# Softmax sums of each four heads in a tile of their own, and their reciprocals written behind the copies of the transposes

## The chip, the core and the metric

The kernel runs on one core of a Trainium2 chip. The metric is the device time of one execution in microseconds (us). Executions of one kernel agree within 0.2% here, most within 0.1%. A single core has no second die to compare with, and all runs below are of the fast state, so times can be set beside each other. Ratios are those of the runs of one round on one chip: the mean time of one kernel's fast runs over the mean of the other's, so they are not quite the ratios of the medians that are quoted.

The engines are called by the profile's short names in its lines: PE is TensorE (PEld its weight loads), DVE VectorE, ACT ScalarE, POOL GpSimd. PSUM is the memory that the matmuls and transposes here write into; the kernel takes it in pieces called banks. The granted clock (PEclk) is the share of its full clock that the profile shows TensorE being given, as a mean over the stretch named.

## The reference, cut to what matters

The first layer is a state-space layer, which the change leaves alone. The second is attention in a 7 x 7 neighbourhood, 12 heads of 32 channels, on a 64 x 64 image, four images:

```python
logits = jnp.stack([jnp.einsum('bnchw,bnchw->bnhw', q, k_pad[..., di:di + H, dj:dj + W])
                    for di in range(ws) for dj in range(ws)], axis=-1)
logits = logits + rel_bias.reshape(nh, ws * ws)[None, :, None, None, :]
attn = jax.nn.softmax(logits, axis=-1)
out = jnp.einsum('bnhwk,bnkchw->bnchw', attn, v_win).reshape(B, C, H, W)
```

The kernel works on blocks of 8 x 16 pixels (128 queries), whose neighbourhoods lie in a window of 14 x 22 = 308 keys. A mask in the bias leaves each query its 49 keys.

## The kernel before

A *turn* handles one group of four heads in one block; there are 4 images x 8 stripes x 4 blocks x 3 groups = 384 turns. What a turn does:

```python
def scores(b, s, bl, m, blk):
    sg = w2.tile([P, 4, NK], F32, tag="sg", ..., bufs=4)
    mx = w2.tile([P, 4], F32, tag="mx", ...)
    for hh in range(4):
        ...
        nc.tensor.matmul(lg[:, :NK], ...)                       # logits into PSUM
        nc.vector.tensor_tensor_reduce(                         # bias, negation, and the maximum
            sg[:, hh, :], lg[:, :NK], bias[:, 4 * m + hh, :], -1.0, BIG,
            ALU.add, ALU.min, mx[:, hh : hh + 1])
        act(sg[:, hh, :], sg[:, hh, :], AF.Exp, scale=-1.0, bias=mx[:, hh : hh + 1],
            accum_out=blk["sum"][:, 4 * m + hh : 4 * m + hh + 1])   # ScalarE: exponential and its sum
    return sg

def normalised(m, sg, blk):
    rs = w2.tile([P, 4], F32, tag="rsum", name="rsum")
    nc.vector.reciprocal(rs, blk["sum"][:, 4 * m : 4 * m + 4])
    for hh in range(4):
        nc.gpsimd.tensor_scalar(sg[:, hh, :], sg[:, hh, :], rs[:, hh : hh + 1], None, ALU.mult)

def weighted(m, sg, blk):
    ta = []
    for pair in range(2):
        pt = bank(ps_t, "pt")                                    # ps_t has two banks
        ...                                                      # four transposes, 128 x 110
        t = w2.tile([P, 4, P], F32, tag="ta", name="ta", bufs=4)
        nc.vector.tensor_copy(...)                               # VectorE empties the bank: "the copies"
        ta.append(t)
    pt = bank(ps_t, "pt")                                        # needs the first bank again
    ...                                                          # four transposes, 128 x 88: "the third set"
    nc.scalar.copy(...)                                          # ScalarE empties it
    return ta, tb
```

The turns overlap. While the scores of group n are made, group n-1 is normalised and group n-2 transposed:

```python
blk["sum"] = w2.tile([P, NH], F32, tag="sum", ..., bufs=3)       # once a block of three groups
for m in range(NJ):
    sg = scores(b, s, bl, m, blk)
    if turned is not None:
        attend()                                                 # attention times values, group n-3
    turned = None
    if pending:
        normalised(*pending[-1][:3])                             # group n-1
    if len(pending) > 1:
        pm, psg, pblk, *rest = pending.pop(0)
        turned = (pm, *weighted(pm, psg, pblk), pblk, *rest)     # group n-2
    pending.append((m, sg, blk, bl, b, s, aT))
    ...                                                          # a piece of the next stripe's projections
```

In this layer the source's order is not the order of the queues: the framework's scheduler sorts each engine's instructions when the program is built.

## Time and profile before

9406.5 us. The prediction below shows the profile's lines and works from them; it takes the attention layer from 6860 us to the end. *Idle* is a stretch's length less TensorE's busy time.

Its lines are to be read from the bottom of the chain: a wait of VectorE costs time only where TensorE, which has the most to do, waits for what stands behind it.

### The profile page before, as it was taken

The numbers are of one execution on the slowest core, as the hardware profiler recorded it, in microseconds if no ns is written. First come the engines' busy times: TensorE is split into PE (matmuls) and PEld (weight loads), VectorE is DVE, ScalarE is ACT, GpSimd is POOL, SyncE is SP. The second block draws the span as 40 slices with busy tenths as digits, with TensorE's granted clock in tenths as the row PEclk, the third lists the DMA queues.
The fourth block names the chain that finished last, engine by engine and source line by source line (L and its number), as shares of the span: only waits on it lengthen the run. The fifth ranks groups of instructions, "written<-read, shape, count | busy, mean of one in ns | idle before, by whom it ended". The sixth has DMA issues, their size and how long they took to land. (4 is left out here: it accounts for less than half of the span.)

```text
span 9402.5 us, 141121 instructions
## 1 busy us (share of the span) xinstructions
PE 7733.7 (82%) x45882; PEld 5668.8 (60%) x45882; DVE 7512.0 (80%) x15604; ACT 5726.1 (61%) x13566; POOL 7641.1 (81%) x6679
## 2 busy tenths in 40 slices
PE   6877787778777887787778877887799999999998
PEld 5666666666666666666666666666554555555555
DVE  6888988898889888889898888888855555556555
ACT  5676666666666676666666666666544444444444
POOL 5898989888989898898889998999856666666666
PEclk8887888788888887788878887888699999999999
DMA  3111111111111111111111111111122222222222
GB/s 98 51 49 60 55 51 44 56 55 51 49 52 61 48 45 53 61 52 48 52 56 49 43 46 57 49 44 45 47 83 83 77 81 77 74 79 79 75 78 61
DMA packets 301925, 558.02 MB, mean 59 GB/s; under 512 B 61916, under 2 KB 185580, under 8 KB 301060
## 3 DMA queue, kind: packets, MB, share of 16 engines
q1 hardware_dynamic: 301188, 549.00, 18.6%
q8 instruction: 364, 5.96, 0.3%
q14 instruction: 373, 3.06, 0.1%
HBM read 446.33 MB, written 84.73 MB: 56 GB/s over the span
## 5 line engine op out<-in xcount | busy, mean ns | idle before, releaser
L96 ACT ACTIVATE da<-dt,nega 128x256 f32<-128x256 f32 x6144 | 2922.9, 477 | 1425.8 <-DVE hs L558 974.7
L538 POOL TENSOR_TENSOR db<-dtx,B 128x1024 f32<-128x1024 f32 x1536 | 3620.7, 2357 | 30.1
L558 DVE TENSOR_TENSOR_SCAN hp<-da,state,db 128x256 f32<-128x256 f32 x2880 | 2154.2, 748 | 303.7 <-POOL state L569 193.3
L558 DVE TENSOR_TENSOR_SCAN hs<-da,state,db 128x256 f32<-128x256 f32 x2880 | 2119.0, 736 | 341.8 <-ACT da L96 341.7
L909 POOL TENSOR_SCALAR sg<-sg,rsum 128x308 f32<-128x308 f32 x1536 | 1603.9, 1064 | 917.1 <-DVE rsum L907 771.1
L570 POOL TENSOR_TENSOR hs<-hs,C 128x512 f32<-128x512 f32 x1536 | 1951.8, 1271 | 123.2 <-POOL state L569 0.8
L578 PE MATMUL y<-ident,hv 128*128 128x128 f32 x6144 | 1191.1, 327 | 954.7 <-DVE hv L565 948.7
L578 PEld LDWEIGHTS y<-ident,hv 128*128 128x128 f32 x6144 | 850.1, 165 | 1396.3 <-DVE hv L565 1280.4
L96 ACT ACTIVATE sg<-sg,mx 128x308 f32<-128x308 f32 x1536 | 830.8, 542 | 872.7 <-DVE mx L894 840.4
L578 PE MATMUL y<-ident,hs 128*128 128x128 f32 x6144 | 1156.2, 321 | 141.5 <-POOL hs L570 140.1
L381 PE MATMUL mm_ps<-xn,w_in 128*128 128x256 f32 x4608 | 1162.6, 404 | 2.0 <-DVE xn L357 2.0
L565 DVE TENSOR_TENSOR hv<-hp,C 128x512 f32<-128x512 f32 x1536 | 1044.5, 680 | 0.0
L578 PEld LDWEIGHTS y<-ident,hs 128*128 128x128 f32 x6144 | 900.6, 169 | 189.4 <-POOL hs L570 186.0
L381 PEld LDWEIGHTS mm_ps<-xn,w_in 128*128 128x128 f32 x4608 | 924.3, 207 | 132.9 <-issue 3.0
L894 DVE CUSTOM_DVE_ANT_0 sg<-lg_ps,bias 128x308 f32<-128x308 f32 x1536 | 653.9, 474 | 270.4 <-PE lg_ps L888 270.0
L569 POOL COPY state<-hs 128x2 f32<-128x2 f32 x1536 | 289.1, 188 | 526.9 <-DVE hs L558 466.8
L388 PE MATMUL mm_ps<-xb,dcv 128*128 128x256 f32 x3072 | 716.5, 379 | 0.0
L388 PEld LDWEIGHTS mm_ps<-xb,dcv 128*128 128x128 f32 x3072 | 567.3, 190 | 72.3
L488 PE MATMUL mm_ps<-xd,w_dt 24*128 24x256 f32 x768 | 332.4, 573 | 293.5 <-DVE yg L605 290.6
L616 PE MATMUL mm_ps<-yg,w_out 128*128 128x256 f32 x2304 | 518.8, 379 | 0.0
L926 DVE COPY ta<-pt_ps 110x512 f32<-110x512 f32 x768 | 490.7, 680 | 33.4 <-PE pt_ps L921 28.4
L936 ACT COPY tb<-pt_ps 88x512 f32<-88x512 f32 x384 | 223.0, 581 | 426.8 <-PE pt_ps L932 422.7
(145 smaller groups left out, 10677.7 us busy)
## 6 DMA issues: line engine op xcount, KB each, us to landing
B<-bcrows SPq DMA_DIRECT2D x256, 512.0 KB
C<-bcrows SPq DMA_DIRECT2D x256, 512.0 KB
vw<-vd SPq DMA_DIRECT2D x1792, 33.0 KB
xr<-x SPq DMA_DIRECT2D x28, 1056.0 KB
vd<-v SPq DMA_DIRECT2D x280, 96.0 KB
xi<-in_x_dram SPq DMA_DIRECT2D x64, 384.0 KB
x<-xo SPq DMA_DIRECT2D x64, 384.0 KB
o<-x SPq DMA_DIRECT2D x96, 256.0 KB
```

The lines of the kernel that those rows point to most:

```text
L96: ins = nc.scalar.activation(o, i, func, **kw)
L381: nc.tensor.matmul(pb[:, k, :], w_in[:, j, m * P : (m + 1) * P], xn[:, j, :], start=(j == 0), stop=(j == NJ - 1),)
L388: nc.tensor.matmul(pb[:, k, :], dcv[:, d, c, :], xb[:, d, c : c + T], start=(c == 0), stop=(c == KC - 1),)
L538: nc.gpsimd.tensor_tensor(db, h["dtx"].unsqueeze(1).broadcast_to([P, NG, T]), h["bc"][g][0], ALU.mult)
L558: nc.vector.tensor_tensor_scan(to[:, k, :], da[:, k, :], db[:, 2 * half + k, :], state[:, d, n + k : n + k + 1] if I % NCHUNK else 0.0, AL ...
L565: nc.vector.tensor_tensor(hv, hp, ct[:, 0:2, :], ALU.mult)
L570: nc.gpsimd.tensor_tensor(hs, hs, ct[:, 2:4, :], ALU.mult)
L578: nc.tensor.matmul(y[:, half, :], t[:, k, half * P : (half + 1) * P], ident, is_transpose=True, start=(first and half == 0), stop=(last an ...
L616: nc.tensor.matmul(h["po", first][:, m - first, :], w_out[:, d, m * P : (m + 1) * P], h["yg"][d], start=(d == 0), stop=(d == ND - 1),)
L894: nc.vector.tensor_tensor_reduce(sg[:, hh, :], lg[:, :NK], bias[:, 4 * m + hh, :], -1.0, BIG, ALU.add, ALU.min, mx[:, hh : hh + 1],)
L909: nc.gpsimd.tensor_scalar(sg[:, hh, :], sg[:, hh, :], rs[:, hh : hh + 1], None, ALU.mult)
L926: nc.vector.tensor_copy(t[: KN[0], :, :].rearrange("p a q -> p (a q)"), pt[: KN[0], :])
```

## The change

Two things were intended. The sums of each group get a tile of their own, so that no reciprocal could be tied to another group's exponentials. And the reciprocals are written behind the transposes and copies, so that VectorE would make the copies before it waits for a sum.

```diff
+                sums = w2.tile([P, 4], F32, tag="sum", name=f"sum_{b}_{s}_{bl}_{m}", bufs=4)
@@
-                        accum_out=blk["sum"][:, 4 * m + hh : 4 * m + hh + 1],
+                        accum_out=sums[:, hh : hh + 1],
@@
-            def normalised(m, sg, blk):
+            def normalised(sg, sums):
                 rs = w2.tile([P, 4], F32, tag="rsum", name="rsum")
-                nc.vector.reciprocal(rs, blk["sum"][:, 4 * m : 4 * m + 4])
+                nc.vector.reciprocal(rs, sums)
@@
-                    blk["sum"] = w2.tile([P, NH], F32, tag="sum", name=f"sum_{b}_{s}_{bl}", bufs=3)
@@
                         turned = None
-                        if pending:
-                            normalised(*pending[-1][:3])
                         if len(pending) > 1:
-                            pm, psg, pblk, *rest = pending.pop(0)
+                            pm, psg, psums, pblk, *rest = pending.pop(0)
                             turned = (pm, *weighted(pm, psg, pblk), pblk, *rest)
-                        pending.append((m, sg, blk, bl, b, s, aT))
+                        if pending:
+                            normalised(*pending[-1][1:3])
+                        pending.append((m, sg, sums, blk, bl, b, s, aT))
```

(Cut: the same renaming at the end of the layer.)

## The prediction

> **What bounds the kernel now.** I first split the span at 6860 us, where the first layer ends and the attention layer begins, with the view that gives the busy time of each engine in a stretch.
>
> ```profile
> core 0: us, PE busy (x) PEld busy (x) DVE busy (x) ACT busy (x) POOL busy (x), PEclk, DMA share, GB/s
> 0.00:6860.00 6860.00, 5412.34 (x26484) 4390.68 (x26484) 6022.18 (x10840) 4569.84 (x10008) 6020.07 (x5074) 0.82 0.16 54
> 6860.00:9402.50 2542.50, 2321.36 (x19399) 1278.10 (x19398) 1489.79 (x4764) 1156.21 (x3558) 1621.01 (x1605) 1.00 0.26 75
> ```
>
> The first layer, which the diff does not touch, takes 73% of the time (6860 of 9402.5). The attention layer has 2542.5 us for 384 groups of four heads, 6.6 us each. TensorE is busy in 2321 / 2542 = 91% of it, VectorE in 59%, GpSimd in 64%. So the attention layer belongs to TensorE, and another engine matters only where it makes TensorE wait. Some 221 us are left for that.
>
> Next I asked what the reciprocals (line 907) wait for, and who waits for what in the attention layer.
>
> ```profile
> engine op xcount: duration ns min/median/max, first and last start us, forms
> L907 DVE RECIPROCAL rsum<-sum x384: 159/177/180, 6867.9 to 9380.3; 128x4 f32<-128x4 f32 x192
> ...
>   ACT sg L96: 161.4, 140
> ```
>
> ```profile
> POOL sg L909 <- DVE rsum L907: 771.1, 243, 27.9
> ...
> PE pt_ps L932 <- DVE ta L926: 176.9, 240, 1.7
> ...
> DVE rsum L907 <- ACT sg L96: 161.4, 140, 1.3
> ```
>
> A reciprocal is short (177 ns), but 140 of the 384 hold VectorE idle for 161 us, until ScalarE has delivered the fourth exponential's sum. TensorE sits idle 177 us before the transposes of line 932, because the copies that empty the transposes' PSUM (line 926) are late. That is four fifths of the 221 us. One group in order of time shows that these two rows are one chain:
>
> ```profile
> 8034.06 0.81 PE L826 MATMUL mm_ps<-w_qkv,xn 128*128 128x384 f32 x2
> ...
> 8035.07 0.19 ACT L96 ACTIVATION_READ_ACCUMULATOR sg<-sg,mx 128x1 f32 x1
> ...
> 8035.36 0.18 DVE L907 RECIPROCAL rsum<-sum 128x4 f32<-128x4 f32 x1 [1.25 <-ACT sg L96]
> 8035.46 1.29 DVE L926 COPY ta<-pt_ps 110x512 f32<-110x512 f32 x2
> ...
> 8036.20 0.64 PE L932 MATMUL pt_ps<-ident,sg 128*88 128x128 f32 x4 [1.34 <-DVE ta L926]
> ```
>
> VectorE's last max of the group ends at 8034.10; it then waits 1.25 us for the sum, and the two copies stand behind that wait. TensorE stops for 1.34 us in the same place. The author's aim is plain: put the reciprocal behind the copies, and the copies need not wait for ScalarE.
>
> **The Trainium skill.** "PSUM — Partial Sum Buffer", section "Engine vs sequencer instructions", says that the queues of ScalarE, VectorE and GpSimd are strictly first in, first out. The trace agrees: at 8034.10 the copies' input is there, since the eight transposes end at 8034.2 and the first pair earlier, and they still start only behind the reciprocal. So what decides is the place in VectorE's queue, not what an instruction needs. "Perfetto Trace Analysis", section "Identifying Dependency Chains", says to read off the semaphores an instruction waits on; I did that in the built programs below. "Advanced Engine Details and Errata", section "SBUF Cachelines", gives 16-byte lines. Four float32 sums are 16 bytes: one line as columns 4m to 4m+3 of the old 48-byte tile, and one line as the new tile. I expect nothing from the layout; no run here tests it yet.
>
> **The change part by part.** Nothing is added or removed: 384 reciprocals, 1536 exponentials with a sum and 1536 GpSimd multiplications stand on both sides, in the same shapes.
>
> *The tile of its own.* The old tile held the sums of three groups; one could fear that a reciprocal waits for the next group's exponentials, or the reverse. I took each wait of the 384 reciprocals in the built program and looked up which instruction raises the semaphore to the awaited value. In the program before, all 384 wait for the fourth exponential of their own group; in the changed program, all 384 again. The columns had already been kept apart, so the new tile removes no wait: 384 x 0 = 0 us. The sum tiles take 3 x 64 bytes before and 4 x 32 after, so later tiles move by 64 or 192 bytes; no buffer's number of copies changes.
>
> *The reciprocal behind the copies.* In the source, the reciprocal is now written after the transposes and copies of the older group. But the queues are not in source order: a scheduler sorts them, as TensorE's interleaved order shows. So I compared the built orders. On TensorE, ScalarE, GpSimd and the DMA queue all instructions stand in identical places. On VectorE, with reciprocals taken out, the other instructions are in the same order; of the 384 reciprocals, 383 stand at the same place among them and one moves back by six instructions. It is in the first blocks, where the pipeline fills. In the changed program 128 reciprocals still stand directly in front of the copies, against 129 before. In the trace before, those 129 account for 151 of the 161 us (128 of them waited, 1.18 us on average). So this part reaches 1 of 129 places: 1.2 to 1.4 us at most, and possibly nothing there, because that reciprocal now stands behind a copy that waits for a DMA buffer.
>
> *Waits.* Matching every instruction with its counterpart, the instruction that each wait names is the same except around the moved reciprocal: one wait on GpSimd, two on ScalarE, three on TensorE, one on the DMA queue, eight rows on VectorE. One max near it loses a wait on VectorE itself, which was satisfied long before.
>
> Sum: 0 (layer one) + 0 (tiles) + 0 for 383 reciprocals + about -1 to +1 for one = 0 within 1 us. The timed median is 9406.47 and the profiled run 9404.24, with a spread of 3 us over three runs (0.03%). I predict 9405.
>
> **The rivals.** *The intent comes true.* If the 129 reciprocals really stood behind the copies, the copies would start at about 8034.10 in the group shown, the first pair's PSUM would be free 0.7 us later, before TensorE's two matmuls end (8034.06 + 0.81 = 8034.87), and the 1.34 us would go. The bound is 129 x 1.34 = 173 us, near the 177 us in the row, hence about 9235 us (-1.8%). The reciprocal itself would lose nothing (the copies end at about 8035.4, when its sum has just come), but with TensorE's wait gone the next group's maxima and exponentials, in the same order, can become the next wait, so part would come back: 9235 to 9330. For it: the chain of waits. Against it: the built queue, which is what the engine executes. I give it 2%, for a chip-side program ordered otherwise than the one I built; building both again gave the same order.
>
> *The late reciprocal starves GpSimd.* GpSimd waits 771 us for reciprocals, so a later reciprocal could delay the multiplications and the transposes two groups on. Each group has four multiplications of 1.06 us, 4.2 of 6.6 us, so there are some 2.4 us of slack, and a delay of 1.3 us would fit. With 383 unmoved it cannot appear; if all moved and it did bite, say 0.5 us x 129 = +65 us, 9470, still within 2%.
>
> *Addresses.* Tiles shifted by 64 or 192 bytes might change an access time. A 1% longer exponential (831 us busy) would be 8 us of ScalarE, which has 54% idle time; the effect on the end would be a fraction: within 9400 to 9410.
>
> **Range and chances.** The program is the same but for one instruction, so the range is run spread and chip-to-chip difference, which I estimate at 0.15% either way for want of a second chip: 9390 to 9420. Faster by over 2% would need more than 188 us, more than the intent's whole bound of 173: 0.01. Slower by over 2% has no mechanism: 0.01. Within 2%: 0.98.
>
> **What would show it right or wrong.** Right: VectorE's wait before the reciprocals stays at about 161 us in 140 places, TensorE's idle time before the transposes of line 932 (933 in the new file) at about 177 us, the attention layer at 2542 us, and the same group still shows reciprocal, then copies. Wrong: if the wait on ScalarE falls to a few us and the copies stand in front of the reciprocals, the order I built is not the one that ran. If the order is the same and the time still moves by over 20 us, the sums' layout or the addresses matter, which I hold for free; then the mean of an exponential (542 ns), a sum read (187 ns) or a reciprocal (177 ns) must have moved.

## The result, and the profile after

9408.65 us (median of 4 runs, 9405.86 to 9410.43) against 9406.49 us of the kernel before; the ratio is 1.0002 with a 95% interval of 0.9985 to 1.002. Nothing moved.

The busy times by stretch of the changed kernel, columns as in the prediction:

```profile
0.00:6860.00 6860.00, 5411.45 (x26482) 4396.89 (x26483) 6022.85 (x10840) 4567.89 (x10008) 6013.99 (x5074) 0.82 0.16 54
6860.00:9403.80 2543.80, 2322.53 (x19401) 1279.83 (x19399) 1489.23 (x4764) 1155.92 (x3558) 1617.00 (x1605) 1.00 0.25 75
```

The attention layer takes 2543.8 us against 2542.5, TensorE is busy in 2322.5 of them against 2321.4. Next the waits of the changed kernel in that layer (who waited for whom: us in total, times, longest); its lines stand one lower in the file, so 908 is the reciprocal, 927 the copy, 933 the third set of transposes.

```profile
POOL sg L910 <- DVE rsum L908: 776.4, 240, 27.9
...
PE pt_ps L933 <- DVE ta L927: 177.8, 241, 1.7
...
DVE rsum L908 <- ACT sg L96: 161.7, 139, 1.6
```

All three rows are the ones of before (771.1, 176.9, 161.4). One wait of 140 has gone. The same turn in order of time, in the changed kernel (start, length, engine, what, idle before and its releaser):

```profile
8034.87 0.08 DVE L895 DVE_READ_ACCUMULATOR2_ANT mx<- 128x1 f32 x1
...
8035.91 0.19 ACT L96 ACTIVATION_READ_ACCUMULATOR sg<-sg,mx 128x1 f32 x1
...
8036.20 0.18 DVE L908 RECIPROCAL rsum<-sum 128x4 f32<-128x4 f32 x1 [1.25 <-ACT sg L96]
8036.30 1.29 DVE L927 COPY ta<-pt_ps 110x512 f32<-110x512 f32 x2
...
8037.05 0.64 PE L933 MATMUL pt_ps<-ident,sg 128*88 128x128 f32 x4 [1.34 <-DVE ta L927]
```

VectorE has its last maximum at 8034.95, waits the same 1.25 us, the copies still stand behind the reciprocal, and TensorE waits the same 1.34 us for them.

### The profile page after: what moved, and what is told of

It reads as the page before. It is cut to its first block, busy times and chain, and to the rows that moved or that the text cites. A ratio compares the mean times of both kernels' runs of the same rounds, so it can differ in the third digit from the quotient of the medians.

```text
span 9403.8 us, 141120 instructions
## 1 busy us (share of the span) xinstructions
PE 7734.0 (82%) x45882; PEld 5676.7 (60%) x45882; DVE 7512.1 (80%) x15604; ACT 5723.8 (61%) x13566; POOL 7631.0 (81%) x6679
```

## The experiments

The theory: the change left the queues as they were, and the wait itself is real and worth about what TensorE loses. The chief rival: the wait is hidden, and something else would take its place. A second rival: the two halves of the change cancel each other. To move instructions for certain, the experiments use a tie that the scheduler must keep. It orders two instructions of one engine in its queue and adds no wait:

```python
def queued_behind(ins, earlier):
    if earlier is not None:
        tc.add_manual_dep(ins.ins, earlier.ins.name,
            mybir.DependencyInfo(mybir.DependencyClass.NoSync, mybir.DependencyReason.DATA),
            reason="vector engine order")
    return ins
```

All ten gave correct results. Each was timed in three rounds beside the kernel before; 9408.4 us is its median in the rounds of experiments 1 to 4, 9403.9 in those of 5 to 8, 9406.4 in those of 9 and 10.

### e1: the reciprocal tied behind the copies that stand next to it

In the queues of before, the reciprocal of group n stands beside the copies of group n-2, in 129 of the 384 turns directly in front of them. That had not been seen when the diff was written: the diff swaps the reciprocal of group n-1 with those copies, and the scheduler had long placed that one a turn earlier.

```diff
+            last_ta = [None, None]
-                nc.vector.reciprocal(rs, sums)
+                queued_behind(nc.vector.reciprocal(rs, sums), last_ta[-2])
@@ in weighted
-                    nc.vector.tensor_copy(
+                    copied = nc.vector.tensor_copy(
@@ behind the loop over pairs
+                last_ta.append(copied)
```

> The reciprocal of group n is tied, in VectorE's queue only, behind the copies of group n-2, which is the pair of instructions that stand next to each other in the queue that stalls; in the built program the 128 reciprocals directly in front of copies are then behind them, and TensorE's order changes in 57 of 31,775 places. My theory (the change did nothing because the queue stayed, and the wait itself is real): VectorE's wait before reciprocals falls from 161 us to under 20, TensorE's idle time before the third set of transposes from 177 to under 50 us, and the time to 9235 to 9330 us. Rival (the wait is hidden, another wait takes its place): VectorE's wait falls all the same, but the time stays within 20 us of 9406.

Measured: 9256.9 us, ratio 0.9838 (0.9823 to 0.9853). The rival falls. In this file L922 is the reciprocal, L924 GpSimd's multiplication, L936 the first two sets of transposes, L941 the copy and L948 (L947 in e2) the third set. The row for what the reciprocals wait for, and TensorE's waits in the attention layer:

```profile
  ACT sg L96: 1.5, 3
```

```profile
PE pt_ps L948 <- DVE ta L941: 46.7, 115, 0.8
...
PE pt_ps L936 <- POOL sg L924: 3.8, 6, 1.2
```

161 us of VectorE's wait have become 1.5, and TensorE's wait for the copies 46.7 instead of 176.9: 130 us less of it, of the 151.5 us gained. A turn like the one above, now:

```profile
8043.83 0.08 DVE L895 DVE_READ_ACCUMULATOR2_ANT mx<- 128x1 f32 x1
8043.83 1.28 DVE L941 COPY ta<-pt_ps 110x512 f32<-110x512 f32 x2
...
8044.57 0.64 PE L948 MATMUL pt_ps<-ident,sg 128*88 128x128 f32 x4
...
8044.87 0.19 ACT L96 ACTIVATION_READ_ACCUMULATOR sg<-sg,mx 128x1 f32 x1
...
8045.16 0.18 DVE L922 RECIPROCAL rsum<-sum 128x4 f32<-128x4 f32 x1
```

The copies start at the moment of the last maximum, the transposes no longer carry an idle time, and the reciprocal follows the copies just when its sum has come. It loses nothing by standing behind them.

### e2: the diff's wish taken literally

Here the reciprocal is tied behind the copies that its source line follows in the changed kernel (`last_ta[0]`, the latest, instead of `last_ta[-2]`). Since its own turn's copies are older ones, it moves a whole turn back.

> The literal wish of the diff, enforced: each reciprocal is tied behind the copies that its source line now follows. Those are the copies of the older group of the next turn, so the reciprocal of group n moves a whole turn of some 6.6 us back in the queue. My theory: VectorE's wait falls to about 0 and the copies' wait goes, but GpSimd's four multiplications (4.2 us) then start so late that TensorE's transposes wait for them, some 0.5 to 1 us in many of the 384 turns; the gain of 170 us is eaten in part or whole: 9250 to 9450 us, with a new wait of the transposes on GpSimd of over 50 us. Rival (the wait was hidden): 9406 within 20 us or above.

Measured: 9506.9 us, ratio 1.0105 (1.009 to 1.012): 98 us slower than before and above the 9450 that I had allowed. VectorE's wait is gone (0.8 us, once). The new wait of TensorE is the one expected:

```profile
PE pt_ps L936 <- POOL sg L924: 139.5, 277, 1.2
PE pt_ps L947 <- DVE ta L941: 11.5, 46, 0.8
```

But these waits are not longer than those they replace: TensorE is idle 183 us in this layer, less than the 221 of before. Its busy time grew by 142 us instead, to 2463.1 us for the same matmuls (19,407 recorded against 19,399), and its granted clock over the layer is 0.96 instead of 1.00. One such turn, TensorE alone:

```profile
8242.12 0.43 PE L936 MATMUL pt_ps<-ident,sg 128*110 128x128 f32 x2 [0.36 <-POOL sg L924]
8243.15 0.43 PE L936 MATMUL pt_ps<-ident,sg 128*110 128x128 f32 x2 [0.60 <-POOL sg L924]
8244.18 0.65 PE L936 MATMUL pt_ps<-ident,sg 128*110 128x128 f32 x2 [0.60 <-POOL sg L924]
8244.62 1.91 PE L793 MATMUL mm_ps<-xn,w_qkv 128*128 128x512 f32 x2
```

and two stretches of it with the granted clock, the third number from the right:

```profile
8241.00:8244.40 3.40, 1.84 (x23) 0.91 (x16) 1.61 (x7) 1.81 (x8) 3.13 (x4) 0.98 0.44 127
```

```profile
8244.20:8247.40 3.20, 3.20 (x9) 1.98 (x10) 0.78 (x2) 0.00 (x0) 1.59 (x2) 0.51 0.87 283
```

GpSimd hands over one head at a time, and TensorE waits for each. After 3.4 us in which it was busy 1.84 us (54%), its clock is granted at half for about three microseconds, and two matmuls of 128x512 take 1.91 us where the turns of the kernel before show 1.02. I had named the wait and missed that price.

### e3: every reciprocal in front

`normalised` is called for the own group right behind `scores`, and each copy is tied behind that reciprocal.

```diff
                         sg, sums = scores(b, s, bl, m, blk)
+                        normalised(sg, sums)
@@ in weighted
-                    nc.vector.tensor_copy(...)
+                    queued_behind(nc.vector.tensor_copy(...), last_rs[0])
```

> The opposite: every reciprocal right behind its own group's maxima, and the copies tied behind it, in all 384 turns instead of 129. My theory: VectorE's wait before reciprocals rises from 161 us to 350 to 500 us, TensorE's idle time before the third set of transposes by about 1.3 us in each of some 255 more turns, at most 330 us, so 9500 to 9740 us. Rival (the wait is hidden): within 20 us of 9406 though VectorE waits as much.

Measured: 9624.9 us, ratio 1.023 (1.0214 to 1.0245). VectorE waits 331.7 us in 318 waits (a little under the 350 expected), TensorE's wait for the copies is 317.0 us in 288. With e1 this gives the mean change per waiting reciprocal twice: (9408.4 - 9256.9) / (140 - 3) = 1.11 us on the way down, and (9624.9 - 9408.4) / (318 - 140) = 1.22 us on the way up. The second is not waiting alone: by the last table below, TensorE's idle time grew by 152 us and its busy time by 75, as the granted clock fell to 0.97. Idle time alone is (221 - 91) / 137 = 0.95 us down and (373 - 221) / 178 = 0.85 us up.

### e4: the reciprocal on ScalarE

```diff
+                rs = w2.tile([P, 4], F32, tag="rsum", name="rsum", bufs=3)
+                act(rs, sums, AF.Ln)
+                act(rs, rs, AF.Exp, scale=-1.0)
-                return sg, sums
+                return sg, rs
```

(and no reciprocal on VectorE.)

> The reciprocal leaves VectorE: ScalarE computes exp(-ln(sum)) right behind the four exponentials, two instructions on 128x4. VectorE then has no wait on ScalarE's sums and 67 us less work; ScalarE gets 768 instructions of an estimated 0.2 to 0.3 us, 0.5 us a turn, in a layer in which it is idle 54%. My theory: the copies are never held back, 9230 to 9340 us, near the first experiment. Rival (hidden): within 20 us of 9406; if ScalarE's two instructions delay the next group's exponentials onto the path: above it.

Measured: 9278.7 us, ratio 0.9861 (0.9845 to 0.9878). The two instructions take 205 ns each and bring ScalarE from 1156 to 1293 us busy in the layer, where it has time. TensorE waits for the copies 53.2 us. So most of e1's gain comes without a reciprocal behind the copies, once VectorE no longer waits. That it no longer waits is not enough by itself: in e2 it doesn't wait either.

### e5: a reciprocal in front, but one that needn't wait

The reciprocal of the *previous* group is tied behind the last maximum, and the copies behind it.

```diff
-                    nc.vector.tensor_tensor_reduce(
+                    last_max[0] = nc.vector.tensor_tensor_reduce(
@@ in normalised, called for group n-1 in front of weighted
-                nc.vector.reciprocal(rs, sums)
+                last_rs[0] = queued_behind(nc.vector.reciprocal(rs, sums), last_max[0])
@@ in weighted
-                    nc.vector.tensor_copy(...)
+                    queued_behind(nc.vector.tensor_copy(...), last_rs[0])
```

> A reciprocal stands in front of the copies in nearly all turns, as in the third experiment, but it is that of the previous group, whose sums have long been there, so nothing waits. If the wait is what costs (my theory), VectorE's wait on ScalarE before reciprocals is under 5 us and TensorE's idle time before the third transposes is near the 47 us of the first experiment; GpSimd starts later than in the first and some 1.3 us earlier than in the second, where the transposes waited for it 139 us in pieces of 0.4 to 0.8 us, so that wait should fall to under 60 us: 9250 to 9340 us. Rival (a reciprocal in front of the copies costs by its place alone): above 9400 us, like the kernel before or the third experiment.

Measured: 9369.0 us, ratio 0.9968 (0.9956 to 0.9979), between the two ranges, so that neither my theory nor the rival gave the time. The waits came as expected: none of VectorE for sums, 42.0 us of TensorE for copies, 26.2 us for GpSimd. Where the rest went is seen turn by turn. The maxima start each turn, so their starts give its length. This is the mean over the 32 stripes, in us, worked out from the order of time, by the turn's place among the 12 of a stripe:

```text
place             0     1     2     3     4     5     6     7     8     9    10    11
before         5.15  6.07  6.81  5.50  5.62  3.73  6.86  6.94  6.01  6.36  6.33 13.64
e1             5.15  6.03  6.78  5.46  5.59  3.62  6.16  5.82  6.02  4.94  4.99 13.64
e5             5.79  5.78  9.60  5.56  5.60  3.76  6.60  5.85  6.07  5.03  5.06 13.14
```

e1 gains in places 6, 7, 9 and 10, four turns of twelve: 0.70 + 1.12 + 1.42 + 1.34 = 4.58 us, times 32 is 147 us. In places 7, 9 and 10, e5 gains the same within 0.1 us, though a reciprocal stands in front of the copies. That is what the theory asked; in place 6 it keeps only 0.26 of the 0.70 us. It loses 2.8 us in place 2 and 0.6 in place 0, where the next stripe's projections begin. The ties had made the scheduler re-sort other work as well: without the reciprocals, VectorE's queue differs from before in 563 places, in e1 in 15. The last table below says what kind of time it is: of the 109 us by which e5's attention layer is longer than e1's, 92 are busy time of TensorE. Its granted clock is 0.98, and an estimate from that, (1.00 - 0.98) x 2504.9 = 50 us, covers about half of the 92. One turn in place 2, 16.0 us long, shows a stretch at a lower clock, with columns as in the prediction:

```profile
7102.90:7106.30 3.40, 2.76 (x28) 1.66 (x32) 3.40 (x14) 2.42 (x8) 2.44 (x3) 0.95 0.50 169
7106.30:7123.30 17.00, 17.00 (x72) 8.59 (x65) 7.05 (x20) 5.13 (x16) 10.11 (x9) 0.51 0.13 38
```

TensorE has no idle time in these 17 us and runs them at about half clock. The turn of place 2 that starts at 8143.22 takes 9.4 us at a clock of 1.00, so the clock isn't all. What else the new order costs stays open.

### e6, e7, e8: the halves of the change

e6 is e1 with the old tile; e7 has the new tile alone, with the source order of before; e8 the new source order alone, with the old tile.

> The first experiment with the old tile of twelve sums a block. My theory: the tile has no part in anything; same queues as the first experiment, 9257 us within 10, VectorE's wait under 20 us. Rival (the tile of its own frees a wait that only shows once the order is right): above 9300 us.

> Only the tile of its own, source order as before. Built queues are the same as before in every place. Theory: 9408 us within 6, 140 waits of 161 us. Rival (the two halves of the change cancel each other): more than 20 us from it.

> Only the reciprocals' place in the source, with the old tile. One reciprocal of 384 moves in VectorE's queue. Theory: 9408 us within 6, 139 or 140 waits of 161 us. Rival (the two halves of the change cancel each other): more than 20 us from it, with the opposite sign to the tile alone.

Measured: e6 9252.1 us (ratio 0.984, 0.9825 to 0.9854), e7 9402.8 us (1.0000, 0.9992 to 1.0009), e8 9404.7 us (1.0002, 0.9994 to 1.0011), the last two with 12 runs each. VectorE's waits come to 161.4 us in 140 places in e7 and to 161.6 us in 139 in e8. Neither half does anything, so they don't cancel each other, and e6 has the whole gain of e1 without the new tile.

### e9 and e10: one more turn between scores and transposes

To see what made e2 slow, e9 is e2 with a turn more for GpSimd; e10 is the control, the same on top of e1.

```diff
-                sg = w2.tile([P, 4, NK], F32, tag="sg", name=..., bufs=4)
+                sg = w2.tile([P, 4, NK], F32, tag="sg", name=..., bufs=5)
@@
-                        if len(pending) > 1:
+                        if len(pending) > 2:
```

> The second experiment with one more turn between a group's scores and its transposes (and a fifth buffer for the scores), so that GpSimd has a whole turn more for its four multiplications, though the reciprocal still stands a turn late. If lateness of GpSimd was all that cost there, in waits (139 us) and in the lower granted clock that follows them (0.96 over the attention layer, 0.50 for 3 us behind one such group), then the transposes wait under 20 us for GpSimd, the granted clock is 1.00 and the time falls from 9507 to 9240 to 9300 us, as in the first experiment. Rival (the new order, or the lower clock, costs by itself): above 9400 us.

> The first experiment with the same deeper pipeline. There the transposes wait 4 us for GpSimd, so one turn more should give nothing: 9257 within 10 us, and the 47 us before the third transposes stay, because they come from the length of a copy (0.68 us), not from GpSimd. Rival (GpSimd still holds something up): below 9235 us.

Measured: e9 9236.6 us, ratio 0.9819 (0.9804 to 0.9834); e10 9239.0 us, ratio 0.9822 (0.9805 to 0.9838). The attention layer of e9:

```profile
6860.00:9231.80 2371.80, 2298.49 (x19400) 1280.79 (x19398) 1467.66 (x4764) 1155.17 (x3558) 1609.78 (x1605) 1.00 0.28 80
```

and TensorE's wait for GpSimd in it:

```profile
PE pt_ps L936 <- POOL sg L924: 1.1, 3, 0.6
```

The reciprocal stands as late as in e2, but GpSimd is no longer late for the transposes (1.1 us instead of 139.5), the clock is back at 1.00, and 270 us are gone. So e2 lost its time through GpSimd's lateness, with the clock that followed: with the same deeper pipeline, e10's median is 18 us under e1's, and e9's 270 us under e2's. By the table below, 165 of the 274 us by which the layer shrank from e2 to e9 were busy time and 110 idle time; no run took away the one and left the other. e9 came out 3 us and e10 out 8 us below the ranges that I had given; e10's interval overlaps that of e1, so whether the deeper pipeline adds anything to e1 is open. All of e1, e4, e6, e9 and e10 are at least 1.2% under the kernel before with their whole intervals, e5 0.2%; e9 has the lowest median, 1.8% under the kernel before.

TensorE's time in the attention layer, from the views by stretch, gathers it all (us; idle is length less busy):

| kernel | length | busy | idle | granted clock |
|---|---|---|---|---|
| before | 2542.5 | 2321.4 | 221 | 1.00 |
| changed | 2543.8 | 2322.5 | 221 | 1.00 |
| e1 | 2395.8 | 2305.3 | 91 | 1.00 |
| e2 | 2646.2 | 2463.1 | 183 | 0.96 |
| e3 | 2769.5 | 2396.4 | 373 | 0.97 |
| e4 | 2418.7 | 2318.8 | 100 | 1.00 |
| e5 | 2504.9 | 2397.4 | 108 | 0.98 |
| e9 | 2371.8 | 2298.5 | 73 | 1.00 |
| e10 | 2376.1 | 2294.5 | 82 | 1.00 |

## Why the prediction was right, point by point

**The sum of zeros held.** 9405 was predicted, 9408.65 measured, inside the range of 9390 to 9420 and within the runs' spread of before. The three signs named for it came too: 161.7 us of VectorE's wait, 177.8 us of TensorE's, and the reciprocal still in front of the copies.

**The tile removes no wait.** e7 shows it alone (1.0000), and e6 shows that it isn't needed either when the order is right. The layout that I had called free is free: an exponential with its sum takes 542 ns before and after.

**The source order doesn't move the queue.** e8 shows it alone, with 139 waits instead of 140, the one reciprocal that the built programs had shown to move.

**The wait was real, and the first rival's size was near.** It was bounded by 173 us, with part of it coming back. e1 gained 151.5 us (9408.4 to 9256.9), and 46.7 us of TensorE's wait for copies stayed. The reading of VectorE's queue behind it, by what the Trainium skill's "PSUM — Partial Sum Buffer", section "Engine vs sequencer instructions", says of first-in-first-out queues, was borne out: the copies start behind a reciprocal that waited 1.25 us (before), and at once where they stand in front of it (e1). One detail of that reading was loose: at 8034.10 only the first copy had its input; the eighth transpose ended at 8034.22.

**That rival had a wrong picture of the intent.** It took "behind the copies" for one thing, and gave it 9235 to 9330 us. There are two pairs: the reciprocal and the copies that are neighbours in the queue (groups n and n-2, e1: 9256.9), and the two that the diff swaps in the source (n-1 and n-2, e2: 9506.9). Had the scheduler obeyed the diff as e2 does, the kernel would have been 1.05% slower. The prediction's result didn't rest on this, as the queue stayed.

**The rival of a starved GpSimd was right in kind, wrong in size.** I held that a delay of 1.3 us would fit into the slack of 2.4 us a turn. In e1 the transposes wait only 3.8 us for GpSimd. A whole turn of delay (e2) does not fit: there I had put the rival at +65 us, and it cost 98 us net. The term missing from the estimate is TensorE's busy time at a lower granted clock, 142 us more, while its idle time even fell by 38 us. An estimate from the mean clock, (1.00 - 0.96) x 2646.2, gives 106 of the 142 us to the clock.

## What to carry to other kernels

Where a scheduler sorts the queues, read the built queue and not the source: find which instance of an instruction stands in front of which, and tie exactly that pair. In a first-in-first-out queue an instruction of 0.18 us cost about 1 us here when its input was late, and it may be put behind ready work only as far as its own reader can wait. When an order makes the busiest engine wait often in small pieces, look at the granted clock as well as at the waits.

## What the Trainium skill lacked or had wrong

- "TensorE: Matmul & The Clock Gate", section "HAM oscillation — how this bites in real kernels", gives the rule of no idle gaps over some 3.4 us, and the next section, "A second HAM failure mode: psum-queue depth-cycling", names short idle times in one other kernel without a number for them. Here far shorter waits came before a lower clock: in e2 three of 0.36, 0.60 and 0.60 us, then 0.51 over the next 3.2 us. Nor do these runs give a busy share that decides it. TensorE was busy 2.06 of 3.40 us in the kernel before (from 8034.10 us) and kept 1.00 in the next 3.4 us; it was busy 1.84 of 3.40 us in e2, 2.14 in e3 (from 8020.20) and 2.76 in e5 (from 7102.90), and the next stretch had 0.51, 0.54 and 0.51. In e5 it lasted 17 us, all of them busy. What decides stays open; whether transposes, 1.51 of the 1.84 us in e2, count like other matmuls was not tried.
- "Perfetto Trace Analysis", section "Identifying the Most-Contended Engine", warns of TensorE's busy time because matmuls are pipelined. The runs add a second reason: for the same matmuls it went from 2321 to 2463 us, as the granted clock went from 1.00 to 0.96 (e2).
